# A three-layer graph attention kernel: another order on SyncE's queue, and 14 of 24 tiles picked by matmul in every round of layers 1 and 2

## The chip, the cores and the metric

One core of a Trainium2 chip runs the kernel. TensorE (PE, with its weight loads shown as PEld), VectorE (DVE), ScalarE (ACT) and GpSimd (POOL) compute; SyncE (SP), ACT and POOL ask for DMA transfers. The metric is the device time of the program in microseconds (us), the median of several runs.

## The reference

The graph has 6250 nodes of 64 numbers and 206250 directed edges, sorted by their target. Three layers do the same thing with other weights, and the end is a log-softmax, a sum with the input and a normalization:

```python
def _transformer_conv(x, src, dst, edge_attr, Wq, bq, Wk, bk, Wv, bv, We, Ws, bs):
    q = x @ Wq + bq; k = x @ Wk + bk; v = x @ Wv + bv
    e = edge_attr @ We
    kj = k[src] + e
    alpha = jnp.sum(q[dst] * kj, axis=-1) / jnp.sqrt(jnp.float32(D))
    amax = jax.ops.segment_max(alpha, dst, num_segments=N)
    p = jnp.exp(alpha - amax[dst])
    w = p / jax.ops.segment_sum(p, dst, num_segments=N)[dst]
    msg = (v[src] + e) * w[:, None]
    return jax.ops.segment_sum(msg, dst, num_segments=N) + x @ Ws + bs
...
for i in range(L):            # L = 3
    x = relu(_transformer_conv(x, src, dst, edge_attr, ...))
    if i < L - 1: x = _layer_norm(x, ln_gamma[i], ln_beta[i])
return jax.nn.log_softmax(x, axis=1)      # then x0 + this, normalized
```

## The kernel before

**Units and rounds.** Edges stand in tiles of 128. Six tiles make a chunk (`TC`), four chunks make a unit (`LB`) of 24 tiles, and there are 67 whole units and one small one per layer. The loop `for u in range(NU - 2)` is a round: it works on unit `u` and its neighbours at once, in four quarters `j`. In round `u` TensorE adds up the messages of unit `u-2` (`sums`, L1746, with ACT's copy `part<-ps_g`, L1753, behind it; that copy marks the start of a round in the trace), makes the scores of unit `u-1` (`scores`, L1692, reached through `line.products`), turns the node rows of unit `u` (`turn`, L1679, and ACT's copy L1682), and picks rows for unit `u+1`.

**Two ways to a node row.** An edge needs its source node's row `x[src]`. It is either gathered by POOL (an indirect DMA for each tile, L601, after ACT has copied the tile's indices into `gate`, L633), or picked: DVE makes a one-hot matrix `hot` out of the decoded `keys` (L1335), TensorE multiplies it by the node rows `parts` (L1387, 8 matmuls for two tiles), DVE copies the result into `feat` (L1356) and puts three predicated copies over it (L1359), and ACT swaps halves where they stand wrong (L1346 to L1348). `PICKS` says how many of a unit's 24 tiles are picked: 8 in layer 0, and in layers 1 and 2 by turns 12 (units with an even number) and 14 (odd). `depth` splits a number over the two pairs of chunks: 12 is 3 and 3 steps of two tiles, 14 is 4 and 3. The rest, 12 or 10 tiles, is gathered.

**Layer 0 also sorts.** In layer 0 a second stream of work (`sorter`, a `Move` for each unit) brings the edges of a unit into the order that picking wants and stores three things for the later layers: `eaS` (edge features, features on the partitions), `eaP` (the same, edges on the partitions) and `maskS`. `impress` prepares a `stamp` for a move with two copies on DVE (L1064, L1065), and `index` (L1165, L1167) computes keys and indices in PSUM.

**SyncE's queue.** SP runs its instructions in order, and nearly all loads of a round and its stores stand in that one queue: `feat<-eaP` (768 KB, L570, the edge half of a unit's features), four small `q<-qq` (L1633), four `featT<-eaS` (192 KB each, L1659, one for each chunk of a unit: the lower half of what the scores multiply), `shade<-maskS` (192 KB, L1607), `keys<-keyS` (L1831, 448 KB for 14 picks, 384 KB for 12) and four `part<-part` (16 KB each, L1757: `store`, the partial sums of unit `u-2` into two tables in DRAM by turns, each store behind the earlier one of its table). Of a unit's four `featT` loads the first (`across`) is asked for a round ahead, the other three by `more` at the head of `turn(0)`, `turn(1)` and `turn(2)` of the unit's own round; all four must have landed when the next round opens with the scores. When a group of 512 nodes is complete, `finish` runs beside the rounds, some 12 times in a layer: it loads sums (`both<-part`, `sk<-skS`), computes the nodes' new rows, stores them (`x<-y`, in layer 2 `out<-y`, L1575) and projects them for the next layer (`qq<-qs`, L1442, and `skS<-skip`).

**PSUM.** Tiles come out of pools by tag: `a` and `x` have two buffers, `g`, `s`, `p` and `m` one each. Which instruction stands where is set by the order in which the code is written; nothing is scheduled afterwards.

Of the kernel before, what the change touches and what calls it, by code (L numbers as in the profile page):

```python
# [29 lines left out]
BITS = 5  # L30
FAR = 2.0**100
GS = 4
LB = 4
TC = 6
# [11 lines left out]
HALF = NW // 2  # L46
GC = 16
ROWS = 8
PICKS = ((8,), (12, 14), (12, 14))
LEAD = (3, 1, 1)  # L50
NH = WB // KB

# [377 lines left out]
def main_path(  # L430
# [53 lines left out]
    nc = tc.nc  # L484
# [44 lines left out]
    def ps(tag):  # L529
        return psum.tile([P, 512], F32, tag=tag, name=f"ps_{tag}", bufs={"a": 2, "x": 2}.get(tag, 1))  # L530
# [7 lines left out]
    def placed(layer, k):  # L538

        return k < NT and (layer > 0 or k >= U0)  # L540

    def picked(layer, k):

        if not placed(layer, k) or k < LEAD[layer]:
            return 0
        return 2 if layer == 0 and k <= len(groups) // 2 else PICKS[layer][k % len(PICKS[layer])]

# [500 lines left out]
    class Move:  # L1048
# [10 lines left out]
        def impress(self):  # L1059

            misc, self.pos = marks[self.c0 // GC]
            self.at = (self.c0 % GC) * TC
            spots = slice(self.at, self.at + LB * TC)
            nc.vector.tensor_copy(self.stamp[:, :, :BITS], misc[:, :BITS, spots].rearrange("p r c -> p c r"))  # L1064
            nc.vector.tensor_copy(  # L1065
                self.stamp[:, :, ROW_P : ROW_K + 1], misc[:, BITS:, spots].rearrange("p r c -> p c r")
            )

# [88 lines left out]
        def index(self):  # L1157

            k = self.k
            n = NP  # L1160
            pi = ps("a")[:, : TC * 3 * LB].rearrange("p (t v c) -> p t v c", t=TC, v=3)
            pk = ps("a")[:LB, : n * P].rearrange("c (t h e) -> c t h e", t=n, h=2)
            those = self.to[:, : n * P].rearrange("p (t h e) -> p t h e", t=n, h=2)
            for h in range(2):
                nc.tensor.matmul(pk[:, :, h], keyc[:, h], those[:, :, h], start=True, stop=True)  # L1165
            for t in range(TC):
                nc.tensor.matmul(  # L1167
                    pi[:, t].rearrange("p v c -> p (v c)"),
                    self.to[:, t * P : (t + 1) * P],
                    pickc.rearrange("p v c -> p (v c)"),  # L1170
                    start=True,
                    stop=True,
                )
            mine = src_b[:, k * LB * TC : (k + 1) * LB * TC]
            nc.vector.tensor_tensor(
                mine.rearrange("p (c j t) -> p t c j", j=2, t=TC),
                pi[:, :, 0].rearrange("p t (c j) -> p t c j", j=2),
                shift.unsqueeze(2).to_broadcast([P, TC, LB // 2, 2]),
                ALU.add,
            )  # L1180
            nc.vector.tensor_scalar(mine, mine, N - 1, None, ALU.min)
            for h in range(2):
                there = slice(h * P // 2, (h + 1) * P // 2)
                nc.vector.tensor_copy(kbs[there, k], pi[there, :n, 1 + h])
            key = small.tile([LB, n, P], FP16, name="key", bufs=1)
            nc.scalar.copy(key.rearrange("c t e -> c (t e)"), pk.rearrange("c t h e -> c (t h e)"))
            nc.scalar.dma_start(keyS[k].rearrange("t c e -> c t e"), key)
            moved.add(k)
# [597 lines left out]
    chunks = {}  # L1786
# [38 lines left out]
    def decode(layer, k):  # L1825

        n = picked(layer, k) if k < NT else 0
        if n and (layer, k) not in keys and (layer or k in moved):
            room = max(PICKS[layer]) * P
            keys[layer, k] = stock[0].tile([P, room], FP16, name="keys")  # L1830
            nc.sync.dma_start(  # L1831
                keys[layer, k][:, : n * P],
                keyS[k].rearrange("t c e -> (t c e)")[: n * P].partition_broadcast(P),
            )
# [43 lines left out]
    def step(n=1):  # L1878
        for _ in range(n):
            advance()  # L1880
# [14 lines left out]
    for layer in range(L):  # L1895
        line = Line(layer)
# [7 lines left out]
        for u in range(NU - 2):  # L1904
            this = chunks[layer, u]
            picking = picker.batch(u + 1)
            n = picked(layer, u + 1)
            n //= 2
            pace = 0 if layer else 6 if u < 3 else 3
            while not opened:  # L1910
                move(1)
            line.sums(u - 2)
            line.products(u - 1, 0)
            if waiting:
                active.append(waiting.pop(0))
            for j in range(LB):
                picker.quarter = j
                if j == 2:
                    line.weights(u - 1, 0)
                this.turn(j)  # L1920
                if j == 0:
                    line.refill(u - 2)
                free(u, j)
                if j == 0 and layer:
                    line.most(u - 1, 0)
                    line.products(u - 1, 1, "m")
                if j == 1:
                    line.store()
                    if not layer and placed(0, u + 1):
                        line.most(u - 1, 1)  # L1930
                a, b = -(-n * j // LB), -(-n * (j + 1) // LB)
                if layer:
                    for i in range(max(b - a, 1)):
                        next(picking, None)
                        if not i and not j:
                            line.most(u - 1, 1)
                if j == 0:
                    close_up()
                else:
                    step()  # L1940
                if not layer:
                    move(pace - pace // 2)
                    if j == 0:
                        line.most(u - 1, 0)
                    for _ in range(b - a):
                        next(picking, None)
                    move(pace // 2)
                    picker.evacuate()
                if j == 0:
                    if not layer:  # L1950
                        line.products(u - 1, 1)
                        if not placed(0, u + 1):
                            line.most(u - 1, 1)
                    ask(layer, u + 1)
                    chunks[layer, u + 1].across()
                if j == 2:
                    line.weights(u - 1, 1)
                    chunks[layer, u + 1].shade()
                    decode(layer, u + 2)
            assert next(picking, None) is None  # L1960
            if any(not pair for _, pair, *_ in picker.swaps):
                picker.flush()
            picker.ready.update(keys)
            picker.aim()
            for k in range(u + 2, u + 4):
                decode(layer, k)
# [14 lines left out]
        u = NU - 2  # L1981
# [117 lines left out]
```

## Time and profile before

| what | value |
|---|---|
| time, median of 3 runs | 4365.49 us (4349.52 to 4369.96) |
| the profiled execution's own time | 4357.57 us |
| its span, first to last instruction | 4355.8 us |
| mean granted TensorE clock | 0.926 |
| layer 0's rounds | 187 to 1970 us of the span |
| layer 1's rounds | 2051 to 3137 us |
| layer 2's rounds | 3226 to 4331 us |

A row of a group reads: line, engine, operation, out<-in, shapes, count | busy time, mean ns of one | idle time of the engine just before them, and what ended it. A row of a wait reads: who <- whom: us in total, times, longest. A row of a stretch gives each engine's busy time in it (with the number of instructions), the granted clock PEclk, the DMA engines' busy share and GB/s. A row of the timeline gives start, length, engine, line, operation, count and the idle time before; SPq is SP's queue.

### The profile page before, as it was taken

The page shows a single profiled execution, that of the slowest core. Times are in us where ns is not written, and L with a number is a line of the kernel's source. Part 1 is how long each engine was busy: PE and PEld are TensorE (multiplying, and loading weights), DVE is VectorE, ACT ScalarE, POOL GpSimd, SP SyncE. Part 2 cuts the span into 40 slices and gives each one's busy share as a digit, 9 for nine tenths or more (in the row PEclk, how much of TensorE's full clock was granted, in tenths as well). Part 3 has the DMA queues.
Part 4 walks back from the last instruction along what each step waited for, and adds up shares of the span by engine and source line. Part 5 has one row for each costly group of instructions (what it writes and reads, how often), then busy time and mean ns, then how long its engine had stood idle before and what let it go on. Part 6 is the DMA issues. An engine that isn't in the chain of part 4 may idle for free.

```text
span 4355.8 us, 108102 instructions
## 1 busy us (share of the span) xinstructions
PE 3555.1 (82%) x34711; PEld 2476.2 (57%) x34711; DVE 3376.9 (78%) x11892; ACT 2305.6 (53%) x5860; POOL 2706.5 (62%) x2642
## 2 busy tenths in 40 slices
PE   4788888888889898985888888788768878777886
PEld 2345555555555555554666666666556666666664
DVE  6678888888888888865787778787667777777775
ACT  1345555555555555553555555555545556555555
POOL 5467665656666665654776666666367666666662
PEclk9889999999999999997999999999879999999997
DMA  5656666656666666665776667766657666666663
GB/s 124 170 167 189 173 179 166 177 155 181 177 165 185 168 173 158 180 174 136 178 188 167 169 172 180 180 167 172 160 133 182 172 170 172 174 161 169 173 171 88
DMA packets 783500, 728.90 MB, mean 167 GB/s; under 512 B 485192, under 2 KB 610050, under 8 KB 782928
## 3 DMA queue, kind: packets, MB, share of 16 engines
q1 hardware_dynamic: 630436, 508.46, 45.5%
q0 software_dynamic: 84224, 86.41, 10.4%
q10 hardware_dynamic: 68268, 127.03, 8.2%
q8 instruction: 283, 4.64, 0.5%
q14 instruction: 289, 2.37, 0.2%
HBM read 562.78 MB, written 158.68 MB: 166 GB/s over the span
## 4 chain that ended last, share of the span: by engine, by line


## 5 line engine op out<-in xcount | busy, mean ns | idle before, releaser
L601 POOL DMA_INDIRECT feat<-x,gate x1460 | 1451.2, 994 | 706.4 <-issue 315.6
L601 POOL DMA_INDIRECT feat<-in_x,gate x1100 | 1181.8, 1074 | 724.0 <-ACT gate L633 421.0
L1387 PE MATMUL ps_x<-parts,hot 128*128 128x256 f32 x6864 | 1033.1, 299 | 173.5 <-DVE feat L1359 157.3
L1387 PEld LDWEIGHTS ps_x<-parts,hot 128*128 128x128 f32 x6864 | 905.8, 199 | 326.7 <-issue 231.2
L1682 ACT COPY featT<-ps_a 64x384 f32<-64x384 f32 x1588 | 753.7, 475 | 538.0 <-PE ps_a L1679 521.9
L1359 DVE COPY_PREDICATED feat<-which,ps_x 128x128 f32<-128x128 int32 x2574 | 779.0, 303 | 88.7
L1335 DVE TENSOR_SCALAR hot<-keys,rank 128x512 fp32r<-128x512 f16 (+1 forms) x1172 | 471.5, 470 | 59.8 <-DMA keys<-keyS 59.2
L1356 DVE COPY feat<-ps_x 128x128 f32<-128x128 f32 x858 | 246.2, 287 | 301.4 <-PE ps_x L1387 295.6
L1679 PE MATMUL ps_a<-ident,feat 128*128 128x128 f32 x2380 | 433.9, 291 | 53.5 <-DMA feat<-x,src_b 31.2
L1692 PE MATMUL ps_s<-featT,q 128*32 128x384 f32 x2134 | 306.3, 505 | 191.2 <-issue 104.6
L1074 DVE TENSOR_SCALAR hit<-ruler,pos 128x384 bf16<-128x384 f16 x1608 | 457.4, 325 | 5.9 <-PE ps_m L1094 5.9
L1679 PEld LDWEIGHTS ps_a<-ident,feat 128*128 128x128 f32 x2380 | 285.1, 147 | 251.6 <-issue 190.2
L1720 ACT ACTIVATE prob<-prob,part 128x768 f32<-128x768 f32 x204 | 190.3, 933 | 251.1 <-DVE part L1719 155.8
L1746 PE MATMUL ps_g<-feat,probT 128*32 128x128 f32 x9672 | 315.3, 276 | 2.0 <-ACT probT L1737 2.0
L1085 PE MATMUL ps_x<-hit,raw 128*64 128x384 bf16 x1608 | 298.7, 367 | 0.1
L1085 PE MATMUL ps_x<-hit,rest 128*64 128x384 bf16 x1608 | 281.1, 346 | 0.0
L1085 PE MATMUL ps_x<-hit,end 128*64 128x384 bf16 x1608 | 280.5, 345 | 0.0
L1746 PEld LDWEIGHTS ps_g<-feat,probT 128*32 128x32 f32 x9672 | 262.9, 111 | 27.8 <-ACT probT L1737 5.7
L1737 ACT COPY probT<-ps_p 128x384 f32<-128x384 f32 x399 | 191.8, 481 | 124.7 <-PE ps_p L1734 78.9
L1734 PE MATMUL ps_p<-ident,prob 128*128 128x128 f32 x1197 | 212.3, 288 | 37.1 <-ACT prob L1720 33.8
L1692 PEld LDWEIGHTS ps_s<-featT,q 128*32 128x32 f32 x2134 | 71.2, 111 | 267.2 <-issue 194.2
L1706 DVE CUSTOM_DVE_ANT_0 prob<-ps_s,shade 128x384 f32<-128x384 f32 x204 | 112.9, 553 | 129.6 <-PE ps_s L1692 120.3
(266 smaller groups left out, 5288.5 us busy)
## 6 DMA issues: line engine op xcount, KB each, us to landing
featT<-eaS SPq DMA_DIRECT2D x792, 192.0 KB
feat<-eaP SPq DMA_DIRECT2D x134, 768.0 KB
raw<-in_ea SPq DMA_DIRECT2D x536, 96.0 KB
eaS<-eT ACTq DMA_DIRECT2D x134, 384.0 KB
eaP<-feat ACTq DMA_DIRECT2D x128, 384.0 KB
shade<-maskS SPq DMA_DIRECT2D x198, 192.0 KB
keys<-keyS SPq DMA_DIRECT2D x66, 448.0 KB
keys<-keyS SPq DMA_DIRECT2D x66, 384.0 KB
```

Source lines behind the costliest of these rows:

```text
L601: nc.gpsimd.indirect_dma_start(out=feat[:, c, t, 0], out_offset=None, in_=xts[layer][:, :], in_offset=bass.IndirectOffsetOnAxis(ap=index[: ...
L1074: nc.vector.tensor_scalar(hit, ruler, self.pos[:, at : at + 1], None, ALU.is_equal)
L1085: nc.tensor.matmul(self.px[j * D : (j + 1) * D, :HE], self.parts[2 * h + i].thirds[part][:, j, t * D : (t + 1) * D], self.hits[h, 2 * i + ...
L1335: nc.vector.tensor_scalar(hot[:, h], keys[self.layer, k][:, first : first + n], rank[:, h : h + 1], None, ALU.is_equal)
L1356: nc.vector.tensor_copy(found, px[:, :, 0])
L1359: nc.vector.copy_predicated(found, which[:, first : first + 2, b].bitcast(I32).unsqueeze(2).to_broadcast([P, 2, D]), px[:, :, b],)
L1387: nc.tensor.matmul(px[:, v].rearrange("p b d -> p (b d)"), hot[:, h, (2 * pair + v) * P : (2 * pair + v + 1) * P], those[:, i, b0 + h * KB ...
L1679: nc.tensor.transpose(pt[:, t * P : (t + 1) * P], rows[:, 2 * t * D : 2 * (t + 1) * D], ident)
L1682: nc.scalar.copy(featT[:, :, h, :], pt[h * D : (h + 1) * D, : n * P].rearrange("d (i e) -> d i e", e=P))
L1692: nc.tensor.matmul(p_s[rows, :w], self.q[:, rows], self.featT[j][:, cols], start=True, stop=True)
L1734: nc.tensor.transpose(p_t[:, t, :n], self.prob[:n, at : at + P], ident[:n, :n])
L1746: nc.tensor.matmul(p_g[rows, :].rearrange("n (h d) -> n h d", h=2), self.probT[:, t, rows], batch[:, j, t], start=(t == 0), stop=(t == sel ...
```

## The change

Five edits, four of them in the order or place of work that stays the same:

1. `PICKS`: in layers 1 and 2 the units with an even number pick 14 tiles too, and gather 10.
2. `line.store()` moves from quarter 1 to the end of quarter 3 of a round.
3. For units whose edges were sorted, `across()` moves from quarter 0 to quarter 2 and `decode` (the keys) stands ahead of `across()` and `shade()` there.
4. `index` puts its tile `pi` into PSUM bank `g` and no longer into `a`.
5. `impress` makes the two copies of `stamp` on ACT and no longer on DVE.

```diff
-PICKS = ((8,), (12, 14), (12, 14))
+PICKS = ((8,), (14,), (14,))
...
-            nc.vector.tensor_copy(self.stamp[:, :, :BITS], misc[:, :BITS, spots].rearrange("p r c -> p c r"))
-            nc.vector.tensor_copy(
+            nc.scalar.copy(self.stamp[:, :, :BITS], misc[:, :BITS, spots].rearrange("p r c -> p c r"))
+            nc.scalar.copy(
                 self.stamp[:, :, ROW_P : ROW_K + 1], misc[:, BITS:, spots].rearrange("p r c -> p c r")
             )
...
-            pi = ps("a")[:, : TC * 3 * LB].rearrange("p (t v c) -> p t v c", t=TC, v=3)
+            pi = ps("g")[:, : TC * 3 * LB].rearrange("p (t v c) -> p t v c", t=TC, v=3)
...
                 if j == 1:
-                    line.store()
                     if not layer and placed(0, u + 1):
                         line.most(u - 1, 1)
...
                     ask(layer, u + 1)
-                    chunks[layer, u + 1].across()
+                    if not placed(layer, u + 1):
+                        chunks[layer, u + 1].across()
                 if j == 2:
                     line.weights(u - 1, 1)
-                    chunks[layer, u + 1].shade()
                     decode(layer, u + 2)
+                    if placed(layer, u + 1):
+                        chunks[layer, u + 1].across()
+                        chunks[layer, u + 1].shade()
+                if j == 3:
+                    line.store()
```

What this does to SP's queue in a round of layer 1 is seen in the built programs. Before, from the last of the four `q` loads on (rows that only repeat, the second pair of stores and the register work between the DMAs, are left out at the marks):

```order
L1633 DMA q_39146<-qq_189 128x32
L1659 DMA featT_39163<-eaS_107 64x768
L1659 DMA featT_39165<-eaS_107 64x768
...
L1757 DMA part0_186<-part_38819 32x130
...
L1757 DMA part1_187<-part_38819 32x130
...
L1659 DMA featT_39200<-eaS_107 64x768
L1607 DMA shade_39248<-maskS_109 128x768
L1831 DMA keys_39288<-keyS_110 128x1536
L1659 DMA featT_39321<-eaS_107 64x768
L570 DMA feat_39329<-eaP_108 128x1536
```

After the change, the same stretch of a round of layer 1:

```order
L1633 DMA q_38784<-qq_189 128x32
L1659 DMA featT_38801<-eaS_107 64x768
L1659 DMA featT_38845<-eaS_107 64x768
L1659 DMA featT_38893<-eaS_107 64x768
L1607 DMA shade_38895<-maskS_109 128x768
...
L1757 DMA part0_186<-part_38472 32x130
...
L1757 DMA part1_187<-part_38472 32x130
...
L1831 DMA keys_38939<-keyS_110 128x1792
L1659 DMA featT_38972<-eaS_107 64x768
L570 DMA feat_38980<-eaP_108 128x1536
```

Before, the first `featT` is the next unit's and the second the running unit's third chunk; the running unit's last chunk comes behind the four stores. Now the running unit's third and fourth chunks come first, the next unit's first chunk third, and the stores stand behind all of them and behind `shade`; the `keys` are those of a unit two rounds on, as before.

On SP in layer 0, where the sorter's `raw` loads stand between, before and then after:

```order
L1659 DMA featT_16307<-eaS_107 64x768
L1659 DMA featT_16309<-eaS_107 64x768
...
L1757 DMA part1_187<-part_15778 32x130
L1033 DMA raw_16375<-in_ea 128x3x64 x2
L1659 DMA featT_16433<-eaS_107 64x768
L1033 DMA raw_16475<-in_ea 128x3x64 x2
L1607 DMA shade_16523<-maskS_109 128x768
L1831 DMA keys_16525<-keyS_110 128x1024
```

```order
L1659 DMA featT_16307<-eaS_107 64x768
L1033 DMA raw_16369<-in_ea 128x3x64 x2
L1659 DMA featT_16427<-eaS_107 64x768
L1033 DMA raw_16469<-in_ea 128x3x64 x2
L1831 DMA keys_16517<-keyS_110 128x1024
L1659 DMA featT_16519<-eaS_107 64x768
L1607 DMA shade_16521<-maskS_109 128x768
L1033 DMA raw_16576<-in_ea 128x3x64 x2
...
L1757 DMA part1_187<-part_15778 32x130
```

Here `keys` moved ahead of one `featT`, of `shade` and of the four stores. The gathers on POOL, counted over the whole program, and the difference:

```order
 L601 DMA feat<-in_x,gate 128x64 x1100
 L601 DMA feat<-x_112,src_b 128x64 x24
-L601 DMA feat<-x_112,gate 128x64 x730
+L601 DMA feat<-x_112,gate 128x64 x664
 L601 DMA feat<-x_113,src_b 128x64 x24
-L601 DMA feat<-x_113,gate 128x64 x730
+L601 DMA feat<-x_113,gate 128x64 x664
```

Each of layers 1 and 2 issues 66 gathers less: 33 units with an even number, two tiles each.

## The prediction

> **What bounds the kernel now.** I read the page's head first, then the layers as stretches, then the rounds, and only then the waits, because three layers with different limits stand in one average.
>
> ```profile
> span 4355.8 us, 108102 instructions
> PE 3555.1 (82%) x34711; PEld 2476.2 (57%) x34711; DVE 3376.9 (78%) x11892; ACT 2305.6 (53%) x5860; POOL 2706.5 (62%) x2642
> ```
>
> No engine is full. The stretches of the three layers' rounds (each engine's busy time, the granted clock, the DMA engines' busy share, GB/s):
>
> ```profile
> 60.00:1970.00 1910.00, 1663.09 (x16259) 994.75 (x16257) 1577.00 (x5600) 1008.30 (x2555) 1162.73 (x1082) 0.94 0.64 171
> 2051.00:3096.00 1045.00, 866.65 (x8674) 686.62 (x8670) 809.08 (x2796) 578.29 (x1511) 702.40 (x707) 0.94 0.69 175
> 3226.00:4270.00 1044.00, 845.40 (x8502) 668.11 (x8495) 807.32 (x2823) 601.42 (x1535) 697.61 (x701) 0.95 0.68 173
> ```
>
> A round opens with ACT's copy L1753, so its first and last start and its count give the mean round, for layers 1 and 2:
>
> ```profile
> L1753 ACT COPY part<-ps_g x63: 266/266/270, 2051.0 to 3083.2; 128x128 f32<-128x128 f32 x63
> L1753 ACT COPY part<-ps_g x63: 266/266/270, 3226.0 to 4258.8; 128x128 f32<-128x128 f32 x63
> ```
>
> That is 1032.2 / 62 = 16.65 us and 1032.8 / 62 = 16.66 us. Single rounds of layer 1 are far from this mean. Here are one with 14 picks, one with 12, and one with 14 that went badly:
>
> ```profile
> 2337.00:2350.70 13.70, 12.48 (x141) 10.42 (x136) 12.30 (x43) 8.61 (x24) 10.33 (x12) 1.00 0.79 215
> 2893.30:2905.50 12.20, 11.50 (x133) 9.45 (x128) 10.58 (x37) 8.46 (x24) 8.38 (x9) 1.00 0.78 217
> 2295.28:2323.09 27.81, 20.92 (x158) 16.27 (x158) 14.82 (x57) 10.16 (x25) 12.70 (x13) 0.75 0.58 142
> ```
>
> The good rounds are nearly filled by PE (12.48 of 13.70 us) and DVE. The bad one has the work of a `finish` in it, but also a lower granted clock (0.75) and holes. Its opening on PE, and SP's queue in the round before:
>
> ```profile
> 2301.91 1.46 PE L1692 MATMUL ps_s<-featT,q 128*32 128x384 f32 x2 [4.26 <-issue]
> ```
>
> ```profile
> 2280.62 0.42 SPq L1442 DMA_DIRECT2D qq<-qs  x1
> 2289.57 2.81 SPq L1633 DMA_DIRECT2D q<-qq  x4
> 2292.49 1.10 SPq L1659 DMA_DIRECT2D featT<-eaS  x2
> 2293.87 4.43 SPq L1757 DMA_DIRECT2D part<-part  x4
> 2298.41 0.48 SPq L1659 DMA_DIRECT2D featT<-eaS  x1
> ```
>
> PE stood 4.26 us before the last scores, at 2301.91. The profile names no releaser ("issue"), but the data it needs is the `featT` that SP asked for at 2298.41, after the round had begun: the queue had waited 8.5 us for `qq<-qs` to land and then spent 4.5 us on the stores. Over each layer, PE's idle time at this one place is
>
> ```profile
> L1692 PE MATMUL ps_s<-featT,q 128*32 128x384 f32 x504 | 85.8, 499 | 75.8 <-issue 48.0 <-DMA featT<-eaS 25.0 <-DMA shade<-maskS 2.8
> L1692 PE MATMUL ps_s<-featT,q 128*32 128x384 f32 x504 | 86.0, 497 | 78.1 <-issue 48.9 <-DMA featT<-eaS 29.2
> ```
>
> in layers 1 and 2, 153.9 us together. SP's own waits in layer 1, and its worst one in layer 2:
>
> ```profile
> SPq L1757 <- DMA part<-part: 121.9, 67, 3.2
> SPq L570 <- PE ps_g L1746: 98.1, 34, 7.8
> SPq L1757 <- DMA feat<-eaP: 70.3, 34, 3.8
> SPq L1633 <- DMA qq<-qs: 54.6, 9, 8.7
> SPq L1575 <- DVE top L1501: 47.6, 5, 10.1
> ```
>
> Only the second is slack: there SP is early and waits for PE. Without it a round of SP costs 16.65 - 98.1 / 62 = 15.1 us, more than the 13.7 us that PE needs in a plain round. So layers 1 and 2 run at the pace of a queue that is a little too long, and PE pays for it at the opening of rounds, because the last thing it needs stands behind four stores that wait for each other.
>
> **The change, part by part.** *Stores last, `featT` first.* The running unit's last `featT` now leaves before the stores: in the bad round at about 2293.6 instead of 2298.41, 4.8 us earlier. PE's wait there was 4.26 us, so most such waits should go; what is left is lateness that the stores did not cause (the 8.5 us for `qq`, the 10.1 us at `out`). Ends: 0, and all 153.9 us. I take two thirds, -103 us. What comes behind the stores instead is `keys` for a unit two rounds on, the next unit's second `featT`, and `feat`: all needed a round later. `finish` reads the stored sums from the next round's first quarter, as before, since it is advanced there only; its first load may now wait for one store (up to 3.2 us by the row), beside other work, so I cost that at nothing; bare, it is 12 x 3.2 = 38 us a layer of SP's time.
>
> *The clock.* The granted clock was 0.94 and 0.95 in these layers, which is 63 + 52 = 115 us of lost clock. In the bad round it sat at 0.75, in the good ones at 1.00, so it goes with the holes. PE is not always on the path: ends 0 and 115, I take half, -57 us. The Trainium skill ("TensorE: Matmul & The Clock Gate", Part 1: The HAM clock gate) says that PE falls to half rate after about 3.4 us of too little activity and needs as long to come back. By that rule filled openings give back the whole 115 us and my sum below would be 58 us lower; the rows agree that the bad rounds are the slow ones.
>
> *Two more picks.* What a step costs in layer 1:
>
> ```profile
> L1387 PE MATMUL ps_x<-parts,hot 128*128 128x256 f32 x3280 | 489.7, 298 | 69.9 <-DVE feat L1359 64.7 <-DVE el L1519 1.5 <-DVE dev L1472 1.5
> L1359 DVE COPY_PREDICATED feat<-which,ps_x 128x128 f32<-128x128 int32 x1229 | 372.1, 303 | 42.3
> L1356 DVE COPY feat<-ps_x 128x128 f32<-128x128 f32 x410 | 117.6, 287 | 124.8 <-PE ps_x L1387 122.0 <-issue 2.1
> L1335 DVE TENSOR_SCALAR hot<-keys,rank 128x256 fp32r<-128x256 f16 x64 | 19.5, 346 | 0.0
> L601 POOL DMA_INDIRECT feat<-x,gate x707 | 703.6, 995 | 342.9 <-issue 153.7 <-ACT gate L633 140.9 <-DMA feat<-x,gate 9.4
> ```
>
> One step is 8 matmuls at 489.7 / 3280 = 0.149 us of PE time each, 1.19 us (the mean of 298 ns overlaps its neighbours), and on DVE 0.287 + 3 x 0.303 + 2 x 0.346 = 1.89 us. It comes 33 times a layer, 66 times: +79 us of PE, +125 us of DVE, and a swap on ACT that is a third longer. POOL loses 132 gathers of about 1 us; since PE waited for a gather only
>
> ```profile
> PE ps_a L1679 <- DMA feat<-x,gate: 6.8, 7, 2.0
> ```
>
> that saves nothing I count. On the path a round goes from the 12.20 us of the row with 12 picks to the 13.70 us of the row with 14: +1.5 us, 66 x 1.5 = +99 us if PE and DVE set the pace in each of these rounds, 0 if the queue covers it. I take three quarters, +74 us, nearer the upper end, since the other edits are meant to uncover exactly this pace. `keys` grows by 64 KB in every second round, and two gathers of 32 KB fall away for it: nothing.
>
> *Layer 0.* Four rows carry its edits:
>
> ```profile
> L1167 PE MATMUL ps_a<-pickc,to 128*128 128x12 bf16 x402 | 20.0, 169 | 50.0 <-ACT key L1186 20.9 <-ACT featT L1682 16.2 <-DVE xT L1434 8.0
> L1335 DVE TENSOR_SCALAR hot<-keys,rank 128x512 fp32r<-128x512 f16 x240 | 102.9, 491 | 57.6 <-DMA keys<-keyS 57.0 <-issue 0.6
> L1065 DVE COPY stamp<-misc 128x72 bf16<-128x72 bf16 x67 | 20.6, 308 | 0.0
> L1064 DVE COPY stamp<-misc 128x120 bf16<-128x120 bf16 x67 | 18.0, 268 | 0.0
> ```
>
> PE waits 50.0 us for a buffer of bank `a` that ACT or DVE still reads; bank `g`'s last user at that place is the copy that opens the round. Ends: 0 and 50 (worse is possible, as `g` has one buffer, and `project` and `finish` use it too). PE is busy 87% of layer 0, so I take 20. DVE waits 57.0 us for `keys`, which now stand ahead of four stores; ends 0 and 57, I take 24. The copies take 38.6 us off DVE and put some such time on ACT, 53% busy there; ends -38.6 and +38.6, as other copies that PE waits for queue behind them; I take -10, since DVE paces only some rounds. Layer 0: -54 us.
>
> The sum: -103 - 57 + 74 - 54 = -140 us. The profiled execution took 4357.6 us (span 4355.8), so 4217.6; the median of the runs lies 7.9 us above it, so 4225 us.
>
> **The rivals.** *A: as above*, mean round 16.65 - 86 / 124 = 15.96 us, 4225 us; with its terms moved by half, 4160 to 4300.
>
> *B: the rounds reach what the queue allows without its slack.* If openings no longer wait, a round costs SP's 15.1 us: (16.65 - 15.1) x 124 = -192, with layer 0 -246: 4119 us. For it speaks that good rounds already take 13.70 us with 14 picks; against it, that no `finish` round did.
>
> *C: the queue stays the bound.* SP issues as many transfers as before, and the stores' waits for each other (121.9 us) stay. A round of SP that never waited for PE:
>
> ```profile
> 2249.40 0.33 SPq L570 DMA_DIRECT2D feat<-eaP  x1
> 2255.18 6.57 SPq L1757 DMA_DIRECT2D part<-part  x4
> 2264.27 0.32 SPq L570 DMA_DIRECT2D feat<-eaP  x1
> ```
>
> It took 14.87 us, and the round of the 8.5 us wait 2300.8 - 2280.2 = 20.6 us. With one such and one slightly longer round in every 5.6, the mean is near 16.4 us: -31 us, and with layer 0's 54, 4280 us. The DMA engines are busy 0.58 to 0.79 in the rounds above, so there is no second queue to flee to inside SP. The Trainium skill ("DMA: Bandwidth & Descriptors", Issuing engines are not separate DMA queues) says that all issuers share the same 16 engines and only issue time is saved by spreading; by that rule an order gives no bandwidth, and C's 4280 us is its time.
>
> *D: slower.* DVE becomes the bound at L1356 to L1359: with 14 picks in each round it carries 12.30 us where a plain round lasts 13.70, and a `finish` round 14.82. If the openings' waits only move to the evacuation of `ps_x` (PE already idles 64.7 us there for `feat` L1359), the picks cost their +99 us, with layer 0's -54 that is +45: 4410 us. It decides from the point at which the openings give back less than 99 / 124 = 0.8 us a round and layer 0 nothing.
>
> **How the numbers follow.** About 0.5% (22 us) is what can be told from no change. Chances: A 0.45, B 0.20, C 0.20, D 0.15. Faster by over 0.5% are A, B and two thirds of C, 0.78; no change the rest of C and a little of D, 0.09; slower 0.13. The range 4110 to 4370 leaves out the lower half of B and most of D.
>
> **What would show it.** L1692's idle time in layers 1 and 2 below 60 us together (A) or still over 120 (C, D); PEclk there at 0.97 or more; L1753's mean round near 16.0, 15.1 or 16.4 us; the wait `feat` L1356 <- `ps_x` or `ps_x` <- `feat` L1359 up by half (D); SP's wait L570 <- PE gone (C) or kept (B); L1167's 50 us and the 57 us for `keys` nearly gone. I am wrong if SP's queue, once nothing holds PE back, turns out the longer of the two everywhere, or if layer 0 is slowed by the copies on ACT.

## The result, and the profile after

The changed kernel takes 4194.6 us (median of 4 runs, 4191.1 to 4198.4), the kernel before 4367.7 us in the runs beside it: 0.961 of it, interval 0.958 to 0.964, 173 us less. Forecast was 4225 us, with 4110 to 4370 as the range. The total came out 30 us from the forecast, but that is partly luck: the experiments below show that the order gave less than was forecast and that the picks cost less, and the two errors cancelled.

From the page of the profiled execution, its span and the engines' busy time:

```profile
span 4195.7 us, 109920 instructions
PE 3513.2 (84%) x35239; PEld 2484.7 (59%) x35239; DVE 3452.3 (82%) x12154; ACT 2347.5 (56%) x5994; POOL 2563.3 (61%) x2510
```

DVE has 75 us more to do than before and PE, with 528 more matmuls, is busy 42 us less. The three layers' rounds as stretches (busy time of PE, PEld, DVE, ACT, POOL, then the granted clock, the DMA engines' share, GB/s):

```profile
60.00:1926.00 1866.00, 1634.05 (x16271) 976.78 (x16269) 1555.55 (x5470) 1042.48 (x2695) 1153.11 (x1082) 0.95 0.67 175
2003.00:3009.00 1006.00, 869.63 (x8955) 702.10 (x8951) 858.75 (x2995) 583.12 (x1513) 637.74 (x645) 0.98 0.75 182
3135.00:4120.00 985.00, 843.75 (x8778) 685.49 (x8769) 856.84 (x3018) 607.74 (x1540) 639.03 (x641) 0.99 0.76 183
```

The clock in layers 1 and 2 went from 0.94 and 0.95 to 0.98 and 0.99. ACT's copy that opens a round, in the two layers:

```profile
L1753 ACT COPY part<-ps_g x64: 266/266/270, 2003.0 to 3003.6; 128x128 f32<-128x128 f32 x64
L1753 ACT COPY part<-ps_g x63: 266/266/271, 3135.4 to 4105.4; 128x128 f32<-128x128 f32 x63
```

The mean round is 1000.6 / 63 = 15.88 us and 970.0 / 62 = 15.65 us, where it was 16.65 and 16.66. Layer 0, counted from its first round to layer 1's, lasts 2003.0 - 190.5 = 1812.5 us, 51 us less than before; layer 1 is 43 us shorter and layer 2, to the end, 69 us. These are differences of single executions, and an experiment below shows that such can be 16 us apart where nothing was changed. PE's idle time ahead of the scores and the largest waits of SyncE's queue, layer 1 and then layer 2:

```profile
L1692 PE MATMUL ps_s<-featT,q 128*32 128x384 f32 x512 | 79.0, 495 | 29.3 <-DMA featT<-eaS 28.7 <-issue 0.4
L1692 PE MATMUL ps_s<-featT,q 128*32 128x384 f32 x504 | 77.6, 489 | 15.0 <-DMA featT<-eaS 12.8 <-DMA part<-part 1.7 <-issue 0.3
```

```profile
SPq L1757 <- DMA part<-part: 152.1, 65, 3.8
SPq L1607 <- DMA feat<-eaP: 66.2, 34, 4.2
SPq L1633 <- DMA qq<-qs: 54.2, 9, 6.3
SPq L570 <- PE ps_g L1746: 15.5, 6, 8.0
...
SPq L570 <- PE ps_g L1746: 9.1, 3, 7.5
```

The openings cost 44 us and no longer 154. SyncE's waits for transfers did not go (`qq` is 54 us, as before, and `part` rose from 121.9 to 152.1), but its wait for PE fell from 98.1 and 84.9 us to 15.5 and 9.1: the queue has hardly any slack now. That is the sign that the prediction had named for its rival C (the queue as the bound), at a mean round near that of its rival A. Three rounds of layer 1, a plain one, one with a part of a `finish`, and a late one:

```profile
2044.00:2057.60 13.60, 12.45 (x142) 10.43 (x138) 12.20 (x43) 8.59 (x23) 10.45 (x11) 1.00 0.80 198
2307.60:2322.90 15.30, 13.71 (x144) 10.73 (x140) 14.05 (x45) 9.14 (x25) 10.50 (x11) 1.00 0.80 185
2338.20:2358.40 20.20, 15.85 (x158) 12.53 (x158) 14.53 (x57) 10.17 (x25) 8.27 (x10) 1.00 0.74 175
```

The first two last as long as DVE is busy plus 1.3 or 1.4 us. The late one follows a round in which SyncE waited 6.3 us for `qq`, as the bad round of the prediction did; its queue, and PE at the opening:

```profile
2335.41 1.15 SPq L1633 DMA_DIRECT2D q<-qq  x2
2336.65 2.08 SPq L1659 DMA_DIRECT2D featT<-eaS  x3
2338.78 0.58 SPq L1607 DMA_DIRECT2D shade<-maskS  x1
2339.61 4.27 SPq L1757 DMA_DIRECT2D part<-part  x4
...
2345.25 0.35 SPq L570 DMA_DIRECT2D feat<-eaP  x1
...
2358.55 0.36 SPq L570 DMA_DIRECT2D feat<-eaP  x1
...
2340.29 0.81 PE L1692 MATMUL ps_s<-featT,q 128*32 128x384 f32 x2 [1.73 <-DMA featT<-eaS]
2341.49 0.80 PE L1692 MATMUL ps_s<-featT,q 128*32 128x384 f32 x2 [0.40 <-DMA featT<-eaS]
```

The four stores still take 4.27 us of the queue, but now behind the `featT` loads; PE stands 1.73 + 0.40 us, not 4.26.

### The profile page after: what moved, and what is told of

Same layout as the page of the kernel before. It is cut to its first block, busy times and chain, and to the rows that moved or that the text cites. A ratio compares the mean times of both kernels' runs of the same rounds, so it can differ in the third digit from the quotient of the medians.

```text
span 4195.7 us, 109920 instructions
## 1 busy us (share of the span) xinstructions
PE 3513.2 (84%) x35239; PEld 2484.7 (59%) x35239; DVE 3452.3 (82%) x12154; ACT 2347.5 (56%) x5994; POOL 2563.3 (61%) x2510
## 4 chain that ended last, share of the span: by engine, by line
## 5 line engine op out<-in xcount | busy, mean ns | idle before, releaser
L601 POOL DMA_INDIRECT feat<-x,gate x1328 | 1318.0, 992 | 729.0 <-ACT gate L633 356.4
L1387 PE MATMUL ps_x<-parts,hot 128*128 128x256 f32 x7392 | 1084.9, 294 | 223.1 <-DVE feat L1359 185.9
L1387 PEld LDWEIGHTS ps_x<-parts,hot 128*128 128x128 f32 x7392 | 946.0, 193 | 383.0 <-issue 213.5
L1359 DVE COPY_PREDICATED feat<-which,ps_x 128x128 f32<-128x128 int32 x2772 | 838.0, 302 | 95.5
L1335 DVE TENSOR_SCALAR hot<-keys,rank 128x512 fp32r<-128x512 f16 (+1 forms) x1304 | 507.3, 457 | 4.7 <-DMA keys<-keyS 4.7
L1679 PE MATMUL ps_a<-ident,feat 128*128 128x128 f32 x2380 | 420.9, 286 | 40.7 <-DMA feat<-x,src_b 31.9
L1356 DVE COPY feat<-ps_x 128x128 f32<-128x128 f32 x924 | 263.9, 286 | 173.6 <-PE ps_x L1387 166.4
L1692 PE MATMUL ps_s<-featT,q 128*32 128x384 f32 x2134 | 289.5, 507 | 81.4 <-DMA featT<-eaS 43.1
L1118 ACT COPY eT<-ps_x 128x384 f32<-128x384 f32 x268 | 129.3, 483 | 122.1 <-PE ps_x L1085 84.7
L1136 ACT COPY feat<-ps_a 128x384 f32<-128x384 f32 x256 | 122.1, 481 | 133.6 <-PE ps_a L1128 97.4
```

What stands on the lines that cost most here:

```text
L601: nc.gpsimd.indirect_dma_start(out=feat[:, c, t, 0], out_offset=None, in_=xts[layer][:, :], in_offset=bass.IndirectOffsetOnAxis(ap=index[: ...
L1335: nc.vector.tensor_scalar(hot[:, h], keys[self.layer, k][:, first : first + n], rank[:, h : h + 1], None, ALU.is_equal)
L1356: nc.vector.tensor_copy(found, px[:, :, 0])
L1359: nc.vector.copy_predicated(found, which[:, first : first + 2, b].bitcast(I32).unsqueeze(2).to_broadcast([P, 2, D]), px[:, :, b],)
L1387: nc.tensor.matmul(px[:, v].rearrange("p b d -> p (b d)"), hot[:, h, (2 * pair + v) * P : (2 * pair + v + 1) * P], those[:, i, b0 + h * KB ...
L1679: nc.tensor.transpose(pt[:, t * P : (t + 1) * P], rows[:, 2 * t * D : 2 * (t + 1) * D], ident)
```

## The experiments

**The parts by themselves.** Four kernels ran beside the kernel before (4365.8 us). The first is the kernel before with one line changed:

```diff
-PICKS = ((8,), (12, 14), (12, 14))
+PICKS = ((8,), (14,), (14,))
```

> Only edit 1: the kernel before, with 14 picks in every round of layers 1 and 2. In the kernel before, SyncE's queue sets most rounds of these layers (mean 16.65 us, where a plain round with 14 picks takes 13.70 us). Theory (the order gave the gain, the picks are paid for by it): openings stay late, L1692's idle time stays near 150 us over both layers, and the 66 added steps cost part of their +99 us of path: 4385 to 4430 us, about 4405. Rival P (the picks are themselves the gain, because 132 gathers fall away and POOL's and the DMA engines' work shrinks): 4290 to 4350. Rival Q (the queue covers the picks wholly): 4368, within 10 us.

Measured: 4380.5 us, 1.003 of before (1.001 to 1.005), 15 us slower. Its rounds in layers 1 and 2:

```profile
L1753 ACT COPY part<-ps_g x64: 266/266/269, 2061.7 to 3109.3; 128x128 f32<-128x128 f32 x64
L1753 ACT COPY part<-ps_g x64: 266/266/269, 3236.7 to 4299.0; 128x128 f32<-128x128 f32 x64
```

16.63 and 16.86 us, against 16.65 and 16.66. The 66 added steps cost about a seventh of the +99 us that they would cost on a free path. That lies between rival Q's range and the one that my theory gave, nearer to Q: on the old order the queue covers most of them. L1692's idle time in layers 1 and 2 is 124 us in this trace and did not stay near 150. Rival P is out.

The second has only the order (here and in the edits below, what stands behind a `#` is a note of mine):

```diff
-                    line.store()               # in quarter 1
...
-                    chunks[layer, u + 1].across()          # in quarter 0
+                    if not placed(layer, u + 1):
+                        chunks[layer, u + 1].across()
...
-                    chunks[layer, u + 1].shade()           # in quarter 2
                     decode(layer, u + 2)
+                    if placed(layer, u + 1):
+                        chunks[layer, u + 1].across()
+                        chunks[layer, u + 1].shade()
+                if j == 3:
+                    line.store()
```

> Only edits 2 and 3: the kernel before, with the stores at the end of a round and with the sorted units' first featT and keys asked for in quarter 2; 12 and 14 picks by turns, as before. Theory: openings and clock come back (the prediction's -103 and -57, and -24 for the keys in layer 0) and nothing pays for more picks: about 4184, 4150 to 4220 us; L1692's idle time in layers 1 and 2 below 60 us. Rival P (most of the gain comes from the picks): 4280 to 4340. Rival R (order and picks need each other: with 12 picks a round is bound by gathers on POOL or by SyncE's queue at some 14 to 15.5 us whatever DVE and PE could do, so 12 picks gain nothing over 14): 4215 to 4250 us.

Measured: 4232.0 us, 0.968 (0.965 to 0.971), 134 us less. That is rival R's time: the order alone gives most of the gain, and less than the 184 us that my terms for it add up to. L1692's idle time is 73 us, not below 60. Layer 0 gave 31 us of it (2019.2 - 187.0 us, from first round to first round) and layers 1 and 2 together 93 us of their profiled spans. Their stretches, PE's idle time at the openings, and the rounds:

```profile
2019.20:3028.00 1008.80, 860.57 (x8700) 680.44 (x8692) 810.90 (x2804) 579.04 (x1512) 705.22 (x711) 0.97 0.76 182
3155.20:4155.00 999.80, 843.25 (x8512) 666.76 (x8505) 808.60 (x2828) 601.97 (x1538) 700.93 (x705) 0.97 0.77 180
```

```profile
L1692 PE MATMUL ps_s<-featT,q 128*32 128x384 f32 x512 | 97.0, 500 | 42.9 <-DMA featT<-eaS 41.6 <-issue 0.9
L1692 PE MATMUL ps_s<-featT,q 128*32 128x384 f32 x504 | 95.7, 494 | 30.4 <-DMA featT<-eaS 27.8 <-issue 1.2 <-DMA part<-part 0.7
```

```profile
L1753 ACT COPY part<-ps_g x64: 265/265/270, 2019.2 to 3021.4; 128x128 f32<-128x128 f32 x64
L1753 ACT COPY part<-ps_g x63: 265/265/270, 3155.2 to 4141.2; 128x128 f32<-128x128 f32 x63
```

The openings gave 154 - 73 = 81 us. The mean round is 15.91 and 15.90 us already, so what the other edits add in these layers is small. PE's busy time in a round is 15.91 x 860.57 / 1008.80 = 13.57 us and 15.90 x 843.25 / 999.80 = 13.41 us, where it was 13.81 and 13.49: some 20 us over both layers. So 81 + 20 us of PE's time account for the 93 us, within the scatter of single executions.

The third has only layer 0's edits:

```diff
-            pi = ps("a")[...]
+            pi = ps("g")[...]
...
-            nc.vector.tensor_copy(self.stamp[...], misc[...])      # both copies
+            nc.scalar.copy(self.stamp[...], misc[...])
```

> Only edits 4 and 5: the kernel before, with index's tile in PSUM bank g and impress's two copies on ACT. Both touch layer 0 alone. Theory (the prediction's -20 and -10): about 4338 us, 4325 to 4350, and layer 0's rounds 30 us shorter together. Rival: these two do nothing that counts, layer 0's gain came from the keys standing ahead of the stores: 4368, within 8 us. Other rival: ACT now delays copies that PE waits for, 4375 to 4395 us.

Measured: 4358.2 us, 0.997 (0.995 to 0.999), 8 us less, between the theory and the first rival, and layer 0 is 14 us shorter in its trace (2043.3 - 193.8 us). Its two waits of layer 0, and below the mark the same two of the changed kernel:

```profile
L1167 PE MATMUL ps_g<-pickc,to 128*128 128x12 bf16 x402 | 20.4, 170 | 13.6 <-DVE y L1540 9.5 <-DVE skip L1448 2.4 <-ACT part L1753 1.8
L1335 DVE TENSOR_SCALAR hot<-keys,rank 128x512 fp32r<-128x512 f16 (+1 forms) x248 | 104.4, 482 | 71.9 <-DMA keys<-keyS 71.7
...
L1167 PE MATMUL ps_g<-pickc,to 128*128 128x12 bf16 x402 | 20.4, 170 | 9.9 <-DVE y L1540 8.2 <-DVE skip L1448 1.7
L1335 DVE TENSOR_SCALAR hot<-keys,rank 128x512 fp32r<-128x512 f16 (+1 forms) x248 | 103.6, 478 | 4.7 <-DMA keys<-keyS 4.7
```

The wait for bank `a` falls from 50.0 to 13.6 us as forecast, but DVE's wait for `keys` grows from 57.0 to 71.9 us: the likely reason is that the kernel gets there earlier and the keys do not. With the order alone the two are 39.4 and 3.6 us; only with both edits do both waits go. Layers 1 and 2 of this kernel, which hold the same instructions as before, took 16 us longer in the profiled execution (4364.0 - 2043.3 against 4355.8 - 2051.0): differences of that size between single executions mean nothing here.

The fourth is the changed kernel with the picks by turns again:

```diff
-PICKS = ((8,), (14,), (14,))
+PICKS = ((8,), (12, 14), (12, 14))
```

> The changed kernel without edit 1: 12 and 14 picks by turns again, with all else changed. The difference to the changed kernel (4194.6 us) is the price of the added picks on the new order. Theory by the prediction's term of +74 us for the picks: about 4121 us, 4100 to 4150. Rival R (rounds with 12 picks are then bound by SyncE's queue or the gathers, so that the picks are free): 4185 to 4205 us. Rival P (with fewer gathers the picks are a gain also here): 4215 to 4260 us.

Measured: 4208.4 us, 0.963 (0.960 to 0.966). The changed kernel is 14 us below it and the intervals overlap: on the new order the added picks are free, if not a small gain. The time lies just above rival R's range (picks free) and below rival P's (picks a gain); the theory by my +74 us missed by 87 us. Against the order alone, layer 0's edits give 24 us here where they give 8 us on the old order, but these intervals overlap too, and in the traces layer 0 itself is 17 and 14 us shorter by them, so the two can't be told apart. Two rounds of layer 1 that follow each other, and PE's waits of the two layers for the openings and for gathers:

```profile
2464.50:2476.70 12.20, 11.49 (x132) 9.38 (x126) 10.75 (x38) 8.43 (x23) 9.46 (x10) 1.00 0.86 230
2476.70:2496.90 20.20, 15.89 (x146) 11.42 (x146) 13.30 (x47) 8.83 (x25) 11.34 (x13) 0.92 0.75 174
...
PE ps_s L1692 <- DMA featT<-eaS: 37.9, 23, 5.8
PE ps_a L1679 <- DMA feat<-x,gate: 13.5, 12, 2.9
...
PE ps_s L1692 <- DMA featT<-eaS: 34.8, 19, 5.5
PE ps_a L1679 <- DMA feat<-x,gate: 10.1, 6, 3.6
```

A round with 12 picks does take 12.20 us, as the prediction read it, but the next one is late. Over both layers, from the starts of L1753, every second round averages 15.0 us (the 12.20 us round is one of these) and the others 16.8; in the changed kernel both kinds average 15.7 to 15.8. What the short round saves is waited for behind it: 24 us for gathers (0.7 us in the changed kernel) and 73 us for `featT` (42 us).

**One step further.** The changed kernel with one step of two tiles more:

```diff
-PICKS = ((8,), (14,), (14,))
+PICKS = ((8,), (16,), (16,))
```

> The changed kernel with 16 picks in every round of layers 1 and 2 and 8 gathers, one step of two tiles more than now (1.9 us more of DVE, 1.2 us more of PE a round). In the changed kernel a round lasts about DVE's busy time plus 1.3 us (13.6 us with 12.2 of DVE, 15.3 with 14.0). On a chip where the kernel before takes about 4366 us, theory (DVE sets the pace of nearly all rounds at 14 picks already): +1.2 to 1.9 us a round, 124 rounds, 4330 to 4430 us. Rival (SyncE's queue and the gathers still set the mean, picks go on being nearly free): 4170 to 4230 us. On the chip where the kernel before takes 5658 us, where 12 picks took 5782 us and 14 about 5456 us (264 gathers less, 1.23 us each): theory (there the gathers set the pace) 5100 to 5250 us; rival (DVE is the bound there too): 5430 us or more.

Measured beside the kernel before at 4365.8 us: 4308.2 us, 0.986 (0.983 to 0.989), 114 us above the changed kernel, a little below my range and far above the rival's. Its stretches, a plain round, the mean rounds, and SyncE's wait for PE in layer 1:

```profile
2014.00:3020.00 1006.00, 882.88 (x9032) 738.03 (x9025) 897.22 (x3091) 566.23 (x1446) 492.04 (x489) 0.97 0.69 174
3194.00:4200.00 1006.00, 859.77 (x8957) 718.24 (x8949) 907.11 (x3154) 593.35 (x1484) 498.75 (x492) 0.99 0.71 173
...
2089.70:2104.80 15.10, 13.66 (x150) 11.45 (x146) 13.61 (x47) 8.78 (x24) 7.77 (x9) 1.00 0.72 182
```

```profile
L1753 ACT COPY part<-ps_g x61: 265/265/267, 2014.2 to 3016.0; 128x128 f32<-128x128 f32 x61
L1753 ACT COPY part<-ps_g x61: 265/265/267, 3194.2 to 4187.6; 128x128 f32<-128x128 f32 x61
```

```profile
SPq L570 <- PE ps_g L1746: 128.5, 40, 8.0
```

16.70 and 16.56 us a round, 0.82 and 0.91 more than with 14, where I had expected 1.2 to 1.9; a plain round went from 13.60 to 15.10. DVE is busy 89 and 90% of these stretches, and PE waits at the openings for 0.1 us at most. SyncE's wait for PE, 15.5 us with 14 picks, is 128.5 us: here the queue has slack and the engines set the pace, DVE above all (over both stretches PE waits 215 us for DVE's copies L1359, DVE 78 us for PE's `ps_x`). So 14 lies close to the point where the two limits meet.

**Runs on a slower machine.** Later, on three chips, the kernel before took 5658 to 5669 us; one of those chips had run it in 4366 us earlier. The ratios of these runs are compared among themselves only. Five kernels ran there, one of them three times, but neither the changed kernel itself nor one with 12 and 14 picks on the new order. Most of the times that were expected for them are for a kernel before at 4366 us, so these runs decide neither those theories nor their rivals. The changed kernel with the stores in quarter 1 again:

```diff
                 if j == 1:
+                    line.store()
...
-                if j == 3:
-                    line.store()
```

> The changed kernel with edit 2 undone: the stores stand in quarter 1 again, ahead of the running unit's fourth featT, with the picks, edit 3 and layer 0's edits kept. Theory (PE waits for the featT that stands behind four stores, and SyncE in turn waits for PE at feat L570, a loop that the late stores open): L1692's idle time in layers 1 and 2 back from 44 us to 110 or more, SyncE's wait L570 <- PE back from 25 us to 130 or more, 4270 to 4330 us. Rival K (the place of the keys and of the first featT carried the gain): 4190 to 4220 us.

> The kernel of the earlier run with edit 2 undone (stores in quarter 1 again), once more, since the four runs beside that one fell on a chip where the kernel before takes 5658.7 us and where SyncE mostly waits for PE. On a chip where the kernel before takes about 4366 us, theory (the stores ahead of the fourth featT make openings late, and SyncE and PE wait for each other in turn): 4270 to 4330 us, L1692's idle time in layers 1 and 2 at 110 us or more, SyncE's wait L570 <- PE 130 us or more. Rival K (edit 3 carried the gain): 4190 to 4220 us.

> The same kernel a third time (edit 2 undone: stores in quarter 1, ahead of the running unit's fourth featT; all else as changed), for a chip on which the kernel before takes about 4366 us; the two runs so far came out at 0.966 of the kernel before on a chip where that takes 5658 us and SyncE is not the bound. Theory: 4270 to 4330 us, L1692's idle time in layers 1 and 2 at 110 us or more, SyncE's wait L570 <- PE at 130 us or more. Rival K (edit 3 carried the gain): 4190 to 4220 us. If the kernel before takes 5658 us again: 0.966 once more, as the order of the stores plays no part there.

Measured: 5475.2, 5469.7 and 5485.0 us, 0.967, 0.966 and 0.968 of the kernel before. The first two intervals reach from 0.963 to 0.969, the third, for which 0.966 was expected in this case, from 0.965 to 0.970. The changed kernel with edit 3 undone:

```diff
-                    if not placed(layer, u + 1):
-                        chunks[layer, u + 1].across()
+                    chunks[layer, u + 1].across()          # in quarter 0
...
+                    chunks[layer, u + 1].shade()           # in quarter 2
                     decode(layer, u + 2)
-                    if placed(layer, u + 1):
-                        chunks[layer, u + 1].across()
-                        chunks[layer, u + 1].shade()
```

> The changed kernel with edit 3 undone: across and decode where they stood before, the stores last, picks and layer 0's edits as changed. SyncE then asks for the next unit's first featT ahead of the running unit's third and fourth. Theory (the stores' place carries layers 1 and 2; edit 3 gives something in layer 0 only, where keys wait behind other loads): layers 1 and 2 within 15 us of the changed kernel, layer 0 longer by 0 to 25 us, 4195 to 4235 us. Rival K (edit 3 carries the gain): 4270 us or more.

Measured: 5456.6 us, 0.965 (0.961 to 0.969). A little of the openings is left to see even there: PE's idle time at L1692 over layers 1 and 2 is 21 to 24 us in the three runs with the stores early and 8 us here, where they are late and edit 3 is undone. The changed kernel with `qq` in two tensors:

```diff
-    qq = dram.tile([P, (NB + 1) * P], F32, name="qq")
+    qqs = [dram.tile([P, (NB + 1) * P], F32, name=f"qq{i}") for i in range(2)]
...
-        nc.sync.dma_start(qq[...], qs[...])
+        nc.sync.dma_start(qqs[layer % 2][...], qs[...])
...
-                nc.sync.dma_start(self.q[...], qq[...])
+                nc.sync.dma_start(self.q[...], qqs[self.layer % 2][...])
```

> The changed kernel with qq held in two DRAM tensors by turns, one for the layer that reads it and one for the layer that is being prepared, so that a load of q no longer waits for a finish's store to land. In the changed kernel that wait of SyncE is 54.2 us in layer 1 (9 times, up to 6.3 us) and 12.0 us in layer 0. Theory (SyncE's queue still sets the rounds): layer 1 shorter by most of it, 4140 to 4165 us. Rival (PE and DVE set the pace now, and such waits are covered): 4185 to 4200 us.

Measured: 5434.2 us, 0.960 (0.958 to 0.963). With this and the last two stores of a round moved behind `refill` (the bodies of `half` and of the new `store` are left out):

```diff
...
                 if j == 0:
                     line.refill(u - 2)
+                    line.store(False)      # stores 2 and 3 of the unit
...
                 if j == 3:
-                    line.store()
+                    line.half()            # stores 0 and 1 of the unit
```

> The changed kernel with two things taken off SyncE's queue: qq in two DRAM tensors by turns (no load of q waits for a finish's store), and the last two of a round's four stores moved behind the next feat L570, so that a store no longer stands waiting for the one two places ahead of it (SyncE's wait at part<-part is 152 us a layer in the changed kernel). Theory (SyncE's queue still sets the mean round of 15.8 to 16.0 us, while PE and DVE need 13.6 to 15.3): 54 us of layer 1 and a part of the 150 us of each layer come back, 4060 to 4150 us on a chip where the kernel before takes about 4366. Rival (DVE and PE set the pace in most rounds, and the queue's waits are covered): 4180 to 4200 us. Other rival (what stands behind the moved stores is late instead, as the q loads are needed at once): above 4200 us.

Measured: 5461.1 us, 0.965 (0.962 to 0.968). And with 12 picks in every round:

```diff
-PICKS = ((8,), (14,), (14,))
+PICKS = ((8,), (12,), (12,))
```

> The changed kernel with 12 picks in every round of layers 1 and 2 (12 gathered tiles each). The step from 12 and 14 by turns to 14 always took 13.8 us off on this order. Theory (rounds are now paced by SyncE's transfers, which 12 picks do not shorten, and by gathers, of which there are more): another 10 to 30 us above 12 and 14 by turns, 4215 to 4240 us. Rival (only the alternation hurts, since a short round is followed by a late one; even rounds are free to run at the 12.2 us that PE and DVE need): 4100 to 4170 us.

Measured: 5781.6 us, 1.020 (1.017 to 1.023). Where the stores, the keys and `qq` stand makes little difference there (0.960 to 0.968), while 12 picks for 14 cost some 325 us for 264 gathers more (5781.6 - 5456.6, the second being the kernel with edit 3 undone). In the kernel with `qq` in two tensors and split stores, SyncE's longest waits in a stretch of 1000 us of layer 1 are (its line numbers are one higher from the sums on)

```profile
SPq L570 <- PE ps_g L1747: 357.5, 40, 17.2
SPq L570 <- PE ps_m L1693: 34.0, 4, 12.3
SPq L570 <- PE ps_a L1680: 31.2, 3, 12.2
```

In the kernel with edit 3 undone, the queue waits 40.5 us for `part` and 12.1 us for `qq` in such a stretch; here it is 6.5 us for `part` and nothing for `qq`, and the time is no lower, since the queue waits for PE in any case. What holds PE is seen in a round of the kernel with 12 picks, inside the sums:

```profile
2668.87 0.85 PE L1746 MATMUL ps_g<-feat,probT 128*32 128x128 f32 x20
2670.15 0.27 PE L1746 MATMUL ps_g<-feat,probT 128*32 128x128 f32 x1 [0.43 <-issue]
2670.85 0.27 PE L1746 MATMUL ps_g<-feat,probT 128*32 128x128 f32 x1 [0.43 <-issue]
2671.58 0.27 PE L1746 MATMUL ps_g<-feat,probT 128*32 128x128 f32 x1 [0.46 <-issue]
```

Single matmuls come 0.7 us apart there, while POOL gathers; in the changed kernel's trace at 4195.7 us this line hardly waits (2.4 us in all). Over the whole program PE idles 797 us ahead of this line with 12 picks and 486 us in the kernel with edit 3 undone: 310 of the 346 us between the two profiled executions. Why these matmuls stand apart is open.

## Why the prediction was right, and where it was wrong

*Openings, -103 us: right, as idle time.* Idle time at L1692 fell by 81 us with the order alone and by 110 us with everything. The place, the `featT` behind four stores, is seen in the queue of the late round above. Edits 2 and 3 were undone one at a time only on the slower machine, where the queue is no limit, so how the gain of layers 1 and 2 divides between them stays open.

*The clock, -57 us: mis-sized for the order, and not a term by itself.* The clock came back in part with the order alone (0.94 and 0.95 to 0.97, so by the same sum 60 of the 115 us are still lost), but PE's busy time fell by some 20 us only. The step that failed is "63 + 52 = 115 us of lost clock": a share of the span counts the time in which PE stood idle too, and there a low clock costs nothing. The bound should have been made from PE's busy time in good and bad rounds. With everything changed the clock is 0.98 and 0.99, and PE is busy 13.73 and 13.41 us a round, some 10 us less over both layers although 62 more steps of picks stand in these rounds. By the rows of good rounds a step takes PE 12.48 - 11.50 = 0.98 us, so as an estimate some 70 us came back at equal work, and paid for a part of what the picks cost. The Trainium skill ("TensorE: Matmul & The Clock Gate", Part 1: The HAM clock gate) ties a low clock to idle windows, and the trace agrees in so far as the clock is 0.75 in the bad round and 1.00 in the good ones; the 115 us, which the prediction drew from that rule, did not come back in full.

*Two more picks, +74 us: the step that failed.* Price and place were right (12.20 us with 12 picks, 13.60 with 14), but "three quarters, nearer the upper end, since the other edits are meant to uncover exactly this pace" was wrong: +15 us on the old order, -14 us on the new. The other edits did not uncover PE's and DVE's pace as a mean. The changed kernel's plain rounds run at it, but late rounds stand between them, and the mean of 15.88 and 15.65 us is near SyncE's: without its wait for PE a round of SyncE takes 15.6 and 15.5 us. SyncE's slack was used up, not left over, with 12 and 14 picks by turns as with 14 always. That is rival C's mechanism, with a smaller price. C's 16.4 us was put together from single rounds of the old order (20.6 us for one with the `qq` wait, 14.87 for a plain one, and one "slightly longer", which would have to be 17.7 us to give this mean); in the late round above SyncE took 13.3 us from one `feat` to the next (2345.25 to 2358.55). Rival B's 15.1 us, which took SyncE's other waits as fixed, was nearer, but the wait for `part` grew. The likely picture is a loop on the old order (PE late by `featT`, `feat` late by PE, the queue late by `feat`) that the new order opens. No run shows it by itself, and that the queue is the limit is read from its waits: the kernels that shorten the queue ran on the slower machine only. The Trainium skill ("DMA: Bandwidth & Descriptors", Issuing engines are not separate DMA queues) says that DMAs from all issuers run on the same 16 engines; no run here moves a transfer to another issuer, so none tests it. What the order gave was waiting and not bandwidth: about the same bytes (728.9 and 729.0 MB in the whole program) moved in less time, and so the GB/s rose from 175 to 182 in layer 1.

*Layer 0, -54 us: right,* 51 us in the trace. The keys' 24 us and the other edits' 30 us were taken as separate. The waits show that they are not quite, since the wait for `keys` grows where the one for bank `a` goes; the times are too close to tell.

*Rival D (slower through DVE) did not decide.* Its two waits in layer 1 of the changed kernel:

```profile
DVE feat L1356 <- PE ps_x L1387: 63.5, 157, 3.7
PE ps_x L1387 <- DVE feat L1359: 78.6, 97, 1.8
```

The first fell from 122 us, where D had it rise by half; the second rose from 64.7 us only (in layer 2 from 90.7 to 103.1). D's mechanism is real one step on: 16 picks cost 114 us.

In sum, the order was forecast at 160 us in layers 1 and 2 and gave 93; the picks were forecast at +74 and cost about nothing. The errors are 67 us and some 60 to 90 us and have opposite signs. That the total was met so closely is luck.

## What to carry to other kernels

When a queue and the compute engines limit the rounds by turns, set their paces side by side. Here the engines' pace is DVE's busy time of a round plus 1.3 us, and SyncE's the round without its wait for PE, 15.5 to 15.7 us on the new order with up to 14 picks. On that order the engines' pace is about 14.1 us with 12 and 14 picks by turns, 14.9 with 14 and 16.2 with 16 (estimates from the stretches): the step to 14 stayed below the queue's pace and was free, the step to 16 passed it and cost 114 us. The queue's wait for the engines tells afterwards which side has slack (15 us with 14 picks, 128 with 16 in layer 1). The fastest single rounds do not show what a saving is worth: see whether the round behind them is late. A clock below one is lost time only as far as the engine's own busy time shrinks when it returns.

## What was unexpected

One and the same program took 4366 us and some 5660 us, on one chip both at different hours. Single instructions of the versions that ran slowly lasted as long as in the runs at 4366 us on DVE, ACT and POOL (a predicated copy L1359 0.30 us, the copy L1753 0.27, a gather 0.94); the granted clock was 0.83 to 0.87, where the kernel before has 0.93 at 4366 us. In that condition gathers were the dear resource (325 us for 264, 1.23 us each). By that price the 132 gathers that edit 1 takes away are worth 162 us, as an estimate, of the some 200 us by which the versions with 14 picks were faster than the kernel before: there the picks, and not the order, seem to make most of the gain, which no run of the change without edit 1 shows.
